# A four-part reordering in a one-core transformer kernel: keys before the first queries, other room for the last probabilities, operand steps queued with the splits, a deferred factor

## The chip, the cores and the metric

The kernel runs on one core of a Trainium2 chip. The metric is the device time of one execution in microseconds (us). TensorE is called PE, VectorE DVE, ScalarE ACT, GpSimd POOL and SyncE SP, as in the profile.

## The reference

x has 2 sequences of 1024 tokens of width 512. Four blocks follow one another, each with a layer norm ahead of it and a residual around it: a chunked linear attention with decay, a feed-forward block with 8-bit codes as weights, a softmax attention, and the same feed-forward block again.

```
x = x + attn_a(_layernorm(x))
x = x + ffn(_layernorm(x))
x = x + attn_b(_layernorm(x))
x = x + ffn(_layernorm(x))
# attn_a, per chunk of 128 tokens and head of 128:
k = k / max(norm(k), 1e-12)
attn = (q k^T) * beta * decay                 # causal
y = attn v + (q state) * chunk_decay
state = state * total_decay + v^T (k * beta * decay_to_end)
# attn_b: softmax((Q K^T) / sqrt(512)) V, then W_o
# ffn:    W_down (silu(W_gate x) * (W_up x)), W = (codes - 128) * scale
```

## The kernel before, in words

**Products.** A float32 product is made as three products of a rounded type: each operand is split into a high and a low part. `split` (L83 to L86) casts the high part on ACT (L85) and subtracts it from the source on DVE, or on POOL where it is told so, for the low part (L86). `mm3` (L97 to L100) issues high by high (L98), high by low (L99) and low by high (L100). `load_split` (L88) loads a 128x512 block of a weight into a stage tile and splits it. `product_operands` and `weight_product` make two products of weights: M from WqT and WkT at the very start, and V from WvT and Wo at the end of the first attention. `spill` (L181) takes such a product from PSUM: for each of its four blocks it makes two tiles, splits into them and writes both to DRAM; for M the two tiles of each block have the tag sWk, which has two buffers and which the keys of the first attention use too.

**First attention.** 16 tiles of 128 tokens, in four stages of four. At the start, while M is made, tiles 0 to 3 are normalised and turned on PE (`ln_tile`, pxT_a at L133). Then come load_wab (L367, the gates' weights), the constants, Wq from a staged tile (the room y of the pool for turned x), M's spill, the four heads of queries of stage 0 (`q_head`, pq) with tiles 4 to 7 normalised between them, Wk and Wv, and `kv_tile(0)` (L536): the keys and values of a tile, pWk and pWv, biased into sWk and sWv on DVE (L547). For each tile, `k_norm` (L551) squares the keys on ACT (sq, L558), sums them (ss, L560) and bounds the sum (L561) on DVE, takes a power on POOL (s, L563), multiplies it by two factors on DVE (L564, L569) and by the keys on POOL (kw, L571). `scores` (L576) turns the keys on PE (pkT, L581, copied to kT on ACT, L583), makes the state's increment (pd, L594, from sWv and kw), the scores (pS, L609), and weighs them by the factor s and the decay into at (L613). `chunk_out` (L619) makes the output: pl (L628) from sWv and at, pg (L633) from the state. The decay's rows reach all partitions by loads of row (L531), and dec is their exponential (L523).

**What runs beside it.** `fill` puts into each tile's step the normalisation of later stages, the down weights of the feed-forward block, the loads of V's operands, and steps of `combine` (L244), which makes sums and differences of blocks of x (B and T, split by L86 and differenced at L259) for the products of the feed-forward block. V's product is made in the last two tiles' steps (pV, L98 to L100).

**Second attention, its end.** `probs_T` (L997) turns a tile of probabilities: tile 14 on PE (split at once), the others on DVE (py), which then write it to DRAM and read it back in four transfers into the low tile ptl, to be split in place by `probs_split` (L1031). pth is the high part. ptl and pth have two buffers, and so has pe, the tile of probabilities before it is turned. `out_b` (L1038) makes the output pob from these and the values. After the last tile's turned probabilities come six steps of combine("g", 0), then out_b of tiles 13 and 14, the loads of the next block's weights wcg (`stationary`), and out_b of 15.

**What sets the order.** The program is written as one thread; a scheduler with a timeline of its own puts each engine's instructions into one fixed order, by what is free in its timeline and by the program's order. `behind` (L76) says that instructions stand after given others in that order. Each engine then runs its list in order and waits at the head of it. A tile that takes a buffer waits until all readers of the buffer's earlier tile are done, a transfer out included.

Of the kernel before, what the change touches and what calls it, by code (L numbers as in the profile page):

```python
# [16 lines left out]
P = 128  # L17
D = 512
KD = D // P
T = 1024  # L20
# [14 lines left out]
def hybrid_block_kernel(ctx: ExitStack, tc: tile.TileContext, a, out):  # L35
# [313 lines left out]
    with ExitStack() as actx:  # L349
# [2 lines left out]
        a3 = actx.enter_context(tc.tile_pool(name="attn_a3", bufs=3))  # L352
        sp = actx.enter_context(tc.tile_pool(name="stage", bufs=4))

        normed, key_copy = {}, []
        xTa, aba, gta, sca, qTa, kva, ata, deca, sta, rowa, facta = ({} for _ in range(11))
        wqkv = {}
        wab = a1.tile([P, KD, 48], F32R, name="wab")
# [6 lines left out]
                nc.sync.dma_start(out=dst, in_=a["rows"][n:m].partition_broadcast(P))  # L365

        def load_wab():  # L367
            stg = sp.tile([P, 512], F32, tag="stg", name="stg_ab")
            ab = stg[:, 0 : KD * 8].rearrange("p (k c) -> p k c", k=KD)
            nc.sync.dma_start(out=ab, in_=a["Wab"].rearrange("(k p) c -> p k c", p=P))  # L370
            for c in (0, 32):
                split(wab[:, :, c : c + 8], wab[:, :, c + 8 : c + 16], ab)
            nc.vector.tensor_scalar(
                wab[:, :, 16:32], ident[:, 0 : KD * 16].rearrange("p (k c) -> p k c", k=KD), 0.0, None, ALU.mult
            )

        def load_wqkv(nm, staged=None):
            two = [slot(f"{nm}{n}") for n in range(2)]
            wqkv[nm] = [two[k // 2][:, k % 2 * 1024 : (k % 2 + 1) * 1024] for k in range(KD)]
            for k in range(KD):  # L380
                w, eng = wqkv[nm][k], nc.gpsimd if k % 2 else None
                if staged is None:
                    load_split(w, sp, a[nm][k * P : (k + 1) * P, :], f"{nm}{k}", eng)
                else:
                    split(w[:, 0:512], w[:, 512:1024], staged[:, k], eng)

        xa = [x_in[t * P : (t + 1) * P, :] for t in range(NT)]

# [144 lines left out]
                in_=cl_d[st][i * H : (i + 1) * H, :].rearrange("h c -> (h c)").partition_broadcast(P),  # L533
            )

        def kv_tile(t):  # L536
            st, i = divmod(t, ST)
            xh, xl = xTa[st]
            cs = bass.ts(i, P)
            kv = []  # L540
            for nm, b in (("Wk", bk_b), ("Wv", bv_b)):
                ps = psum(f"p{nm}{t}")
                for k in range(KD):
                    w = wqkv[nm][k]
                    mm3(ps, xh[:, k, cs], xl[:, k, cs], w[:, 0:512], w[:, 512:1024], k == 0, k == KD - 1)
                o = tl(f"s{nm}", t, pool=a3 if nm == "Wv" else ap)
                nc.vector.tensor_tensor(o.rearrange("p h d -> p (h d)"), ps, b, ALU.add)  # L547
                kv.append(o)
            kva[t] = kv

        def k_norm(t, after=None):  # L551

            st, i = divmod(t, ST)
            beta, ec, _ = sca[st]
            kf, v = kva[t]
            sq = tl("sq", t)
            with tc.issue_after(after) if after is not None else nullcontext():
                squared = nc.scalar.activation(sq, kf, AF.Square).ins  # L558
            ss = mp.tile([P, H], F32, tag="ss", name=f"ss{t}")
            nc.vector.tensor_reduce(ss, sq, AX.X, ALU.add)  # L560
            nc.vector.tensor_scalar(ss, ss, 1e-24, None, ALU.max)  # L561
            s1 = mp.tile([P, H], F32, tag="s1", name=f"s1{t}")
            nc.gpsimd.tensor_tensor(s1, ss, mhalf.to_broadcast([P, H]), ALU.pow)  # L563
            scaled = nc.vector.tensor_tensor(s1, s1, beta[:, i, :], ALU.mult).ins  # L564
            normed[t] = squared, scaled
            kw = None
            if t % NC < NC - 1:
                s2 = mp.tile([P, H], F32, tag="s2", name=f"s2{t}")
                scaled = nc.vector.tensor_tensor(s2, s1, ec[:, 1, i, :], ALU.mult).ins  # L569
                kw = tl("kw", t)  # L570
                weighted = nc.gpsimd.tensor_tensor(kw, kf, s2.unsqueeze(2).to_broadcast([P, H, P]), ALU.mult)  # L571
                normed[t] = squared, scaled, weighted.ins
            kva[t] = kf, kw, v
            facta[t] = s1
# [74 lines left out]
        for k in range(KD):  # L649
            if k + 1 < KD:  # L650
                loads.append(product_operands(sp, a["WqT"], a["WkT"], "M", k + 1))
            if k < 2:
                xs += [load_x(xa[t], f"a{t}", "xres" if t > 1 else "xin") for t in (2 * k, 2 * k + 1)]
            if k == 2:

                staged = yp.tile([P, 4, KD, ST, 32], F32, tag="y", name="y_Wq")
                staged = staged.rearrange("p k a b c -> p k (a b c)")
                for m in range(KD):
                    wq_loaded = nc.sync.dma_start(out=staged[:, m], in_=a["Wq"][m * P : (m + 1) * P, :]).ins
            pm, end = next(prep)  # L660
            with behind((end, loads[-1][2])):
                for t in ((), (0, 1), (2, 3), ())[k]:
                    ln_tile(t)
        load_wab()
        load_consts()
        with behind((*normed_x, *parts[-2:])):
            load_wqkv("Wq", staged)
        spill(ap, ("sWk",), pm, m_d, "M")
        for i in range(4):
            q_head(0, i)  # L670
            with behind((wq_loaded,)):
                ln_tile(4 + i)
        load_wqkv("Wk")
        load_wqkv("Wv")
        kv_tile(0)
        decays(0)
        k_norm(0)

# [19 lines left out]
        for t in range(NT):  # L698
            if t + 4 < NT:
                q_head(*divmod(t + 4, ST))  # L700
            if t == 0:
                decay_rows(0)
                load_row(0)
                load_row(1)
            load_row(t + 1)
            if (t + 2) % ST:
                load_row(t + 2)
            if t + 1 < NT:
                kv_tile(t + 1)
            weighed = scores(t)  # L710
            if t + 1 < NT:
                with behind((*normed[t + 1][2:], *key_copy)):
                    decay(t + 1)
            with behind(normed.get(t + 1, (weighed,))):
                for step in fill[t]:
                    step()
                if 1 <= t <= KH:
                    down_weights(sp, t - 1)
                for n in {NT - 3: (0,), NT - 2: (1, 2), NT - 1: (3,)}.get(t, ()):
                    loads.append(product_operands(sp, a["WvT"], a["Wo"], "V", n))  # L720
                if t == NT - 3:
                    first_codes = [
                        load_codes(xp, "xn", a["wgu"][0][:, n * 512 : (n + 1) * 512], f"cf0_{n}") for n in range(2)
                    ]
                if t == NT - 2:
                    wcs.append(stationary(0, "f0", loaded=first_codes))
                for n in range(3 if NT - 4 <= t < NT - 1 else 0):
                    moving.pop(0)()
                if t == NT - 1:
                    wcs.append(stationary(1, "f0", (sp, "stg")))  # L730
            if t == NT - 2:
                prep = weight_product(loads, "V")
            if t >= NT - 2:
                next(prep)
# [145 lines left out]
    with ExitStack() as bctx:  # L880
# [116 lines left out]
        def probs_T(b, i):  # L997
# [4 lines left out]
            if t == NT - 2:  # L1002
# [3 lines left out]
                for s in range(2):  # L1006
                    ps = psum(f"ppt{t}_{s}").rearrange("p (k c) -> p k c", k=4)
                    ks = slice(s * 4, s * 4 + 4)
                    for k in range(4):
                        n = (s * 4 + k) * P  # L1010
                        ends[s] = nc.tensor.transpose(ps[:, k, :], pe[:, n : n + P], ident).ins
                    split(hi[:, ks], lo[:, ks], ps)
                ptT[t] = hi, lo, ri
                return
            y = b1.tile([P, T], F32, tag="py", name=f"py{t}")
            nc.vector.transpose(y, pe)

            nc.sync.dma_start(
                out=p_d[i].rearrange("k p f -> p k f"), in_=y.rearrange("p (k f) -> p k f", k=NK)
# [1 line left out]
            lo = bp.tile([P, NK, P], F32R, tag="ptl", name=f"ptl{t}")  # L1021
            hi = bp.tile([P, NK, P], F32R, tag="pth", name=f"pth{t}")
            raw = lo.bitcast(F32)
            placed = p_d[i].rearrange("k (c j) (r q) -> r j (k c) q", c=4, r=4)
            for r in range(4):
                nc.sync.dma_start(
                    out=raw[32 * r : 32 * (r + 1)].rearrange("p k (c q) -> p (k c) q", c=4), in_=placed[r]
                )
            ptT[t] = hi, lo, ri

        def probs_split(b, i, after):  # L1031
            hi, lo, _ = ptT[b * NK + i]
            with behind(after):
                for s in range(2):
                    ks = slice(s * 4, s * 4 + 4)
                    split(hi[:, ks], lo[:, ks], lo[:, ks].bitcast(F32))

        def out_b(b, i):  # L1038
            t = b * NK + i
            hi, lo, ri = ptT[t]  # L1040
            xr = xp.tile([P, D], F32, tag="xres", name=f"xrb{t}")
            nc.sync.dma_start(out=xr, in_=x2[t])
            po = psum(f"pob{t}")
# [6 lines left out]
        def v_tile(b, kt):  # L1050
# [8 lines left out]
            split(h_, l_, ps)  # L1059
            vs[b, kt] = h_, l_  # L1060

        qs, QA, heads, pes, ptT, vs, last, summed = {}, {}, {}, {}, {}, {}, [], []

        def do(steps, n):
# [92 lines left out]
        array(probs_T, 1, 6)  # L1157
        probs_T(1, 7)
        probs_split(1, 7, last)
        do(moving, 6)  # L1160
        array(out_b, 1, 5)
        array(out_b, 1, 6)
        wcs = [stationary(n, "g0") for n in range(2)]
# [66 lines left out]
```

## Time and profile before

| | |
|---|---|
| median of 3 runs | 955.0 us (953.75 to 956.41) |
| the profiled execution's own time | 955.52 us |
| its span, first to last instruction | 953.8 us |
| mean granted clock of TensorE | 0.996 |
| PE busy | 935.7 us, 98% of the span |
| DVE, ACT, POOL busy | 724.0, 409.8, 223.0 us |
| bytes moved | 162.18 MB, mean 170 GB/s |

The span is cut into busy and idle time for each engine; what an engine waited for at the end of an idle stretch is named as its releaser. The time outside the span, 1.7 us in this execution, is the start and end of the program. A stage is read from its own stretch of the trace, not from the shares of the whole span.

### The profile page before, as it was taken

The page shows a single profiled execution, that of the slowest core. Times are in us where ns is not written, and L with a number is a line of the kernel's source. Part 1 is how long each engine was busy: PE and PEld are TensorE (multiplying, and loading weights), DVE is VectorE, ACT ScalarE, POOL GpSimd, SP SyncE. Part 2 cuts the span into 40 slices and gives each one's busy share as a digit, 9 for nine tenths or more (in the row PEclk, how much of TensorE's full clock was granted, in tenths as well). Part 3 has the DMA queues.
Part 4 walks back from the last instruction along what each step waited for, and adds up shares of the span by engine and source line. Part 5 has one row for each costly group of instructions (what it writes and reads, how often), then busy time and mean ns, then how long its engine had stood idle before and what let it go on. Part 6 is the DMA issues. An engine that isn't in the chain of part 4 may idle for free.

```text
span 953.8 us, 13227 instructions
## 1 busy us (share of the span) xinstructions
PE 935.7 (98%) x4402; PEld 775.3 (81%) x4402; DVE 724.0 (76%) x1457; ACT 409.8 (43%) x795; POOL 223.0 (23%) x318
## 2 busy tenths in 40 slices
PE   8999999998999999999999999999988999999998
PEld 6788888897888878888888888888867788888887
DVE  7657767778999699788947879469873967976655
ACT  4654343344665344454324444145341543534421
POOL 5433323443364011120120402040400261001100
PEclk9999999999999999999999999999999999999999
DMA  9526356665898358632842778226884762573112
GB/s 319 168 95 181 133 140 156 190 187 157 293 370 293 90 188 279 182 83 85 288 113 56 182 172 241 79 45 150 208 236 142 288 192 48 185 263 125 40 61 95
DMA packets 215861, 162.18 MB, mean 170 GB/s; under 512 B 150960, under 2 KB 166640, under 8 KB 215792
## 3 DMA queue, kind: packets, MB, share of 16 engines
q1 hardware_dynamic: 213488, 156.61, 54.0%
q0 software_dynamic: 2304, 4.72, 2.3%
q8 instruction: 35, 0.57, 0.2%
q14 instruction: 34, 0.28, 0.1%
HBM read 104.76 MB, written 41.84 MB: 154 GB/s over the span
## 4 chain that ended last, share of the span: by engine, by line
PE 89%; DVE 3%; DMA 2%; SPq 2%; ACT 1%; issue 1%; POOL 0%; DVEq 0%; ACTq 0%; POOLq 0%
PE pog L852 4%; PE pog L851 4%; PE pof L852 4%; PE pof L851 4%; PE pVg L339 4%; PE pZg L339 4%; PE pXg L339 4%; PE pXf L339 4%; PE pVf L339 4%; PE pZf L339 4%; PE pob L100 3%; PE pob L98 3%; PE pob L99 3%; PE psV L949 2%; PE psZ L949 2%; PE psX L949 2%
## 5 line engine op out<-in xcount | busy, mean ns | idle before, releaser
L851 PE MATMUL pog<-wdg,hsg 128*128 128x512 f32 (+1 forms) x165 | 60.3, 375 | 0.0
L852 PE MATMUL pog<-wdg,hsg 128*128 128x512 f32 (+1 forms) x165 | 60.2, 375 | 0.0
L851 PE MATMUL pof<-wdf,hsf 128*128 128x512 f32 x154 | 59.1, 390 | 0.7 <-ACT hsf L85 0.7
L852 PE MATMUL pof<-wdf,hsf 128*128 128x512 f32 x154 | 58.9, 390 | 0.0
L98 PE MATMUL pob<-vh,pth 128*128 128x512 f32 x128 | 50.8, 397 | 4.3 <-ACT pth L85 4.3
L100 PE MATMUL pob<-vh,ptl 128*128 128x512 f32 x128 | 50.6, 395 | 2.1 <-DVE ptl L86 2.1
L99 PE MATMUL pob<-vl,pth 128*128 128x512 f32 x128 | 50.4, 394 | 0.0
L86 POOL TENSOR_TENSOR hsg<-sgg,hsg 128x128 fp32r<-128x128 f32 x40 | 19.1, 498 | 125.7 <-ACT hsg L85 125.6
L123 POOL TENSOR_TENSOR rs_g<-ve_g,mhalf 128x1 f32<-128x1 f32 x16 | 13.0, 816 | 144.5 <-DVE ve_g L121 144.5
L339 PE MATMUL pXg<-B_g,wcg 128*128 128x512 f32 x176 | 46.6, 389 | 0.0
L339 PE MATMUL pVg<-T_g,wcg 128*128 128x512 f32 x176 | 46.4, 389 | 0.0
L339 PE MATMUL pVf<-T_f,wcf 128*128 128x512 f32 x176 | 46.3, 389 | 0.0
L339 PE MATMUL pXf<-B_f,wcf 128*128 128x512 f32 x176 | 45.4, 390 | 0.0
L123 POOL TENSOR_TENSOR rs_b<-ve_b,mhalf 128x1 f32<-128x1 f32 x16 | 12.7, 802 | 136.8 <-DVE ve_b L121 132.6
L211 POOL DMA_DIRECT2D xT_g<-y_g x48 | 30.9, 652 | 39.7 <-DVE T_b L86 28.5
L339 PEld LDWEIGHTS pVg<-T_g,wcg 128*128 128x128 f32 x176 | 33.0, 188 | 6.9
L339 PEld LDWEIGHTS pXg<-B_g,wcg 128*128 128x128 f32 x176 | 33.0, 188 | 6.9
L339 PEld LDWEIGHTS pVf<-T_f,wcf 128*128 128x128 f32 x176 | 33.1, 188 | 6.9
L339 PEld LDWEIGHTS pXf<-B_f,wcf 128*128 128x128 f32 x176 | 32.9, 188 | 7.0 <-issue 0.3
L851 PEld LDWEIGHTS pog<-wdg,hsg 128*128 128x128 f32 x165 | 31.1, 188 | 5.7
L852 PEld LDWEIGHTS pog<-wdg,hsg 128*128 128x128 f32 x165 | 31.0, 188 | 5.6
L851 PEld LDWEIGHTS pof<-wdf,hsf 128*128 128x128 f32 x154 | 28.9, 188 | 7.1 <-ACT hsf L85 1.1
(333 smaller groups left out, 2738.1 us busy)
## 6 DMA issues: line engine op xcount, KB each, us to landing
wcg<-wc SPq DMA_DIRECT2D x22, 896.0 KB, 6.0
wc<-wcf SPq DMA_DIRECT2D x11, 896.0 KB, 5.9
wcf<-wc SPq DMA_DIRECT2D x11, 896.0 KB, 6.4
p<-py SPq DMA_DIRECT2D x15, 512.0 KB, 3.6
ptl<-p SPq DMA_DIRECT2D x60, 128.0 KB, 3.0
xin_a<-in_x SPq DMA_DIRECT2D x16, 256.0 KB, 4.4
xra<-in_x SPq DMA_DIRECT2D x16, 256.0 KB, 2.8
row<-cl SPq DMA_DIRECT2D x16, 256.0 KB, 3.7
```

The costliest lines, as they stand in the source:

```text
L86: return c.ins, (eng or nc.vector).tensor_tensor(lo, src, hi.bitcast(F32), ALU.subtract).ins
L98: nc.tensor.matmul(ps, lhs_hi, rhs_hi, start=first, stop=False)
L99: nc.tensor.matmul(ps, lhs_hi, rhs_lo, start=False, stop=False)
L100: end = nc.tensor.matmul(ps, lhs_lo, rhs_hi, start=False, stop=last).ins
L123: nc.gpsimd.tensor_tensor(rs, ve, mhalf, ALU.pow)
L211: (nc.sync if sync else nc.gpsimd).dma_start(out=xf[32 * b : 32 * (b + 1), :, c, :], in_=y[32 * c : 32 * (c + 1), b].rearrange("p k i q -> ...
L339: nc.tensor.matmul(ps, w[:, m, k * P : (k + 1) * P], o[:, s, k, :], start=first and k == 0 and s == 0, stop=k == 1 and s == 1, skip_group_ ...
L851: nc.tensor.matmul(ps, hs[i][0][:, j], wd[j][:, ds], start=j == 0, stop=False)
L852: nc.tensor.matmul(ps, hs[i][1][:, j], wd[j][:, ds], start=False, stop=j == KH - 1)
L949: ends[nm] = nc.tensor.matmul(ps, o[:, i, k], w[:, j, k], start=first and k == 0 and i + j == 0, stop=k == 1 and i == 1, skip_group_check= ...
```

## The change

It has four parts. At the start, the staged room holds Wk and not Wq; load_wab has a tile of its own and is called when the third block of M is made; the keys of tile 0 (`kv_part(0, "Wk")`) stand behind the last product of M (`end`), ahead of the first queries; Wq is loaded through the stage tiles. `kv_tile` becomes two calls of `kv_part`. M's spill comes after the keys of tile 0. `k_norm` is cut in two, and of the last tile the second half (`k_factor`) is called in the step of tile 14, behind the last four splits of V's operands. The last tile's probabilities return from DRAM into a tile raw in the room of pe, not into ptl. The six steps of combine("g", 0) stand behind `splits`, the splits of tiles 13 and 14 and the turning of tile 15.

```
@@ -352,7 +352,7 @@
         a3 = actx.enter_context(tc.tile_pool(name="attn_a3", bufs=3))
         sp = actx.enter_context(tc.tile_pool(name="stage", bufs=4))
 
-        normed, key_copy = {}, []
+        normed, key_copy, late_norm = {}, [], []
         xTa, aba, gta, sca, qTa, kva, ata, deca, sta, rowa, facta = ({} for _ in range(11))
         wqkv = {}
         wab = a1.tile([P, KD, 48], F32R, name="wab")
@@ -365,8 +365,7 @@
                 nc.sync.dma_start(out=dst, in_=a["rows"][n:m].partition_broadcast(P))
 
         def load_wab():
-            stg = sp.tile([P, 512], F32, tag="stg", name="stg_ab")
-            ab = stg[:, 0 : KD * 8].rearrange("p (k c) -> p k c", k=KD)
+            ab = a1.tile([P, KD, 8], F32, name="stg_ab")
             nc.sync.dma_start(out=ab, in_=a["Wab"].rearrange("(k p) c -> p k c", p=P))
             for c in (0, 32):
                 split(wab[:, :, c : c + 8], wab[:, :, c + 8 : c + 16], ab)
@@ -380,9 +379,10 @@
             for k in range(KD):
                 w, eng = wqkv[nm][k], nc.gpsimd if k % 2 else None
                 if staged is None:
-                    load_split(w, sp, a[nm][k * P : (k + 1) * P, :], f"{nm}{k}", eng)
+                    _, load = load_split(w, sp, a[nm][k * P : (k + 1) * P, :], f"{nm}{k}", eng)
                 else:
                     split(w[:, 0:512], w[:, 512:1024], staged[:, k], eng)
+            return load if staged is None else None
 
         xa = [x_in[t * P : (t + 1) * P, :] for t in range(NT)]
 
@@ -533,29 +533,40 @@
                 in_=cl_d[st][i * H : (i + 1) * H, :].rearrange("h c -> (h c)").partition_broadcast(P),
             )
 
-        def kv_tile(t):
+        def kv_part(t, nm):
             st, i = divmod(t, ST)
             xh, xl = xTa[st]
             cs = bass.ts(i, P)
-            kv = []
-            for nm, b in (("Wk", bk_b), ("Wv", bv_b)):
-                ps = psum(f"p{nm}{t}")
-                for k in range(KD):
-                    w = wqkv[nm][k]
-                    mm3(ps, xh[:, k, cs], xl[:, k, cs], w[:, 0:512], w[:, 512:1024], k == 0, k == KD - 1)
-                o = tl(f"s{nm}", t, pool=a3 if nm == "Wv" else ap)
-                nc.vector.tensor_tensor(o.rearrange("p h d -> p (h d)"), ps, b, ALU.add)
-                kv.append(o)
-            kva[t] = kv
+            ps = psum(f"p{nm}{t}")
+            for k in range(KD):
+                w = wqkv[nm][k]
+                mm3(ps, xh[:, k, cs], xl[:, k, cs], w[:, 0:512], w[:, 512:1024], k == 0, k == KD - 1)
+            o = tl(f"s{nm}", t, pool=a3 if nm == "Wv" else ap)
+            b = bv_b if nm == "Wv" else bk_b
+            nc.vector.tensor_tensor(o.rearrange("p h d -> p (h d)"), ps, b, ALU.add)
+            kva[t] = (*kva.get(t, ()), o)
+
+        def kv_tile(t):
+            kv_part(t, "Wk")
+            kv_part(t, "Wv")
 
         def k_norm(t, after=None):
 
-            st, i = divmod(t, ST)
-            beta, ec, _ = sca[st]
             kf, v = kva[t]
             sq = tl("sq", t)
             with tc.issue_after(after) if after is not None else nullcontext():
                 squared = nc.scalar.activation(sq, kf, AF.Square).ins
+            normed[t] = (squared,)
+            if t == NT - 1:
+                late_norm.append(lambda: k_factor(t, sq))
+            else:
+                k_factor(t, sq)
+
+        def k_factor(t, sq):
+            st, i = divmod(t, ST)
+            beta, ec, _ = sca[st]
+            kf, v = kva[t]
+            squared = normed[t][0]
             ss = mp.tile([P, H], F32, tag="ss", name=f"ss{t}")
             nc.vector.tensor_reduce(ss, sq, AX.X, ALU.add)
             nc.vector.tensor_scalar(ss, ss, 1e-24, None, ALU.max)
@@ -653,26 +664,28 @@
                 xs += [load_x(xa[t], f"a{t}", "xres" if t > 1 else "xin") for t in (2 * k, 2 * k + 1)]
             if k == 2:
 
-                staged = yp.tile([P, 4, KD, ST, 32], F32, tag="y", name="y_Wq")
+                staged = yp.tile([P, 4, KD, ST, 32], F32, tag="y", name="y_Wk")
                 staged = staged.rearrange("p k a b c -> p k (a b c)")
                 for m in range(KD):
-                    wq_loaded = nc.sync.dma_start(out=staged[:, m], in_=a["Wq"][m * P : (m + 1) * P, :]).ins
+                    nc.sync.dma_start(out=staged[:, m], in_=a["Wk"][m * P : (m + 1) * P, :])
+                load_wab()
             pm, end = next(prep)
             with behind((end, loads[-1][2])):
                 for t in ((), (0, 1), (2, 3), ())[k]:
                     ln_tile(t)
-        load_wab()
         load_consts()
         with behind((*normed_x, *parts[-2:])):
-            load_wqkv("Wq", staged)
+            load_wqkv("Wk", staged)
+        with behind((end,)):
+            kv_part(0, "Wk")
+        wq_loaded = load_wqkv("Wq")
         spill(ap, ("sWk",), pm, m_d, "M")
         for i in range(4):
             q_head(0, i)
             with behind((wq_loaded,)):
                 ln_tile(4 + i)
-        load_wqkv("Wk")
         load_wqkv("Wv")
-        kv_tile(0)
+        kv_part(0, "Wv")
         decays(0)
         k_norm(0)
 
@@ -718,6 +731,9 @@
                     down_weights(sp, t - 1)
                 for n in {NT - 3: (0,), NT - 2: (1, 2), NT - 1: (3,)}.get(t, ()):
                     loads.append(product_operands(sp, a["WvT"], a["Wo"], "V", n))
+                if t == NT - 2:
+                    with behind(parts[-4:]):
+                        late_norm.pop()()
                 if t == NT - 3:
                     first_codes = [
                         load_codes(xp, "xn", a["wgu"][0][:, n * 512 : (n + 1) * 512], f"cf0_{n}") for n in range(2)
@@ -1009,11 +1025,13 @@
                     for k in range(4):
                         n = (s * 4 + k) * P
                         ends[s] = nc.tensor.transpose(ps[:, k, :], pe[:, n : n + P], ident).ins
-                    split(hi[:, ks], lo[:, ks], ps)
-                ptT[t] = hi, lo, ri
+                    splits.extend(split(hi[:, ks], lo[:, ks], ps))
+                ptT[t] = hi, lo, lo.bitcast(F32), ri
                 return
             y = b1.tile([P, T], F32, tag="py", name=f"py{t}")
-            nc.vector.transpose(y, pe)
+            turned = nc.vector.transpose(y, pe).ins
+            if t == NT - 1:
+                splits.append(turned)
 
             nc.sync.dma_start(
                 out=p_d[i].rearrange("k p f -> p k f"), in_=y.rearrange("p (k f) -> p k f", k=NK)
@@ -1021,23 +1039,28 @@
             lo = bp.tile([P, NK, P], F32R, tag="ptl", name=f"ptl{t}")
             hi = bp.tile([P, NK, P], F32R, tag="pth", name=f"pth{t}")
             raw = lo.bitcast(F32)
+            if t == NT - 1:
+
+                raw = bp.tile([P, T], F32, tag="pe", name=f"raw{t}").rearrange("p (k c) -> p k c", k=NK)
             placed = p_d[i].rearrange("k (c j) (r q) -> r j (k c) q", c=4, r=4)
             for r in range(4):
                 nc.sync.dma_start(
                     out=raw[32 * r : 32 * (r + 1)].rearrange("p k (c q) -> p (k c) q", c=4), in_=placed[r]
                 )
-            ptT[t] = hi, lo, ri
+            ptT[t] = hi, lo, raw, ri
 
         def probs_split(b, i, after):
-            hi, lo, _ = ptT[b * NK + i]
+            hi, lo, raw, _ = ptT[b * NK + i]
             with behind(after):
                 for s in range(2):
                     ks = slice(s * 4, s * 4 + 4)
-                    split(hi[:, ks], lo[:, ks], lo[:, ks].bitcast(F32))
+                    done = split(hi[:, ks], lo[:, ks], raw[:, ks])
+                    if b * NK + i == NT - 3:
+                        splits.extend(done)
 
         def out_b(b, i):
             t = b * NK + i
-            hi, lo, ri = ptT[t]
+            hi, lo, _, ri = ptT[t]
             xr = xp.tile([P, D], F32, tag="xres", name=f"xrb{t}")
             nc.sync.dma_start(out=xr, in_=x2[t])
             po = psum(f"pob{t}")
@@ -1059,6 +1082,7 @@
             split(h_, l_, ps)
             vs[b, kt] = h_, l_
 
+        splits = []
         qs, QA, heads, pes, ptT, vs, last, summed = {}, {}, {}, {}, {}, {}, [], []
 
         def do(steps, n):
@@ -1157,7 +1181,8 @@
         array(probs_T, 1, 6)
         probs_T(1, 7)
         probs_split(1, 7, last)
-        do(moving, 6)
+        with behind(splits):
+            do(moving, 6)
         array(out_b, 1, 5)
         array(out_b, 1, 6)
         wcs = [stationary(n, "g0") for n in range(2)]

```

## The prediction, made before the run

> **What bounds the kernel now.** First the page's busy shares and its chain that ended last.
>
> ```profile
> PE 935.7 (98%) x4402; PEld 775.3 (81%) x4402; DVE 724.0 (76%) x1457; ACT 409.8 (43%) x795; POOL 223.0 (23%) x318
> ...
> PE 89%; DVE 3%; DMA 2%; SPq 2%; ACT 1%; issue 1%; POOL 0%; DVEq 0%; ACTq 0%; POOLq 0%
> ```
>
> TensorE (PE) works 98% of the span. So only two things count: what PE waits for, and at what clock it runs. The view of PE's waits comes next (engine, line, whom it waited for: us, times, longest).
>
> ```profile
> PE pob L98 <- ACT pth L85: 4.3, 2, 2.5
> PE pV L99 <- DVE V L86: 2.3, 1, 2.3
> PE pob L100 <- DVE ptl L86: 2.1, 1, 2.1
> PE pab L401 <- DVE wab L86: 1.5, 1, 1.5
> ...
> PE pl L628 <- DVE at L613: 0.5, 1, 0.5
> ```
>
> They sit, by the instruction starts, at 19.5 us (pab, 1.46), 228.4 (pl, 0.54), 231.8 (pV, 2.26), 703.7 (pob, 1.75), 706.1 (pob, 2.07) and 720.5 (pob, 2.52): 10.6 us, and the change aims at each. Then the table of stretches (us, PE busy ... PEclk, DMA share, GB/s):
>
> ```profile
> 231.80:233.94 2.14, 0.03 (x1) 0.00 (x0) 2.14 (x3) 0.00 (x0) 1.61 (x2) 1.00 0.57 166
> 233.94:237.36 3.42, 3.27 (x8) 2.59 (x9) 3.42 (x7) 0.95 (x1) 0.00 (x0) 0.50 0.82 258
> ...
> 708.40:711.81 3.41, 3.41 (x9) 2.64 (x9) 2.68 (x4) 0.69 (x1) 0.00 (x0) 0.50 1.01 334
> ```
>
> After two of the stops the granted clock is 0.50 for 3.41 us; some eight 128x512 products go at 0.427 us apart instead of 0.2275, so each costs 8 x 0.20 = 1.6 us more. All that the change can win is 10.6 + 3.2 = 13.8 us.
>
> Last, the path of tile 1 through the first attention, which the change touches without naming it: the chain, and the timeline of GpSimd (POOL).
>
> ```profile
> 52.50 0.44 PE pkT L581 x4
> ...
> 63.72 0.44 PE pkT L581 x4
> 64.16 0.89 PE pd L594 x8
> ```
>
> ```profile
> 56.89 1.01 POOL L563 TENSOR_TENSOR s<-ss,mhalf 128x4 f32<-128x4 f32 x1 [1.14 <-DVE ss L561]
> ...
> 58.72 1.04 POOL L571 TENSOR_TENSOR kw<-sWk,s 128x512 f32<-128x512 f32 x1 [0.82 <-DVE s L569]
> ```
>
> kw1 is ready at 59.8, and PE wants it (pd1) at 64.0: 4.2 us of slack.
>
> **What the Trainium skill says.** "TensorE: Matmul & The Clock Gate", What's actually happening: the clock is halved after an idle window of 3413 ns, and the windows run free of the kernel. The trace agrees: both drops last 3.413 us and lie 139 windows apart; the windows before them were about 62% and 70% idle; one 46% idle had no drop. [...] the last two writes of M landed 1.98 and 1.97 us after issue. "SBUF — State Buffer", SBUF: two separate sides: a DVE operation with two SBUF inputs and a GpSimd operation lock each other out. The trace agrees: a Wq split took 1.76 us on DVE beside GpSimd's, against 0.69 alone.
>
> **The change, part by part.**
>
> Start. pWk0 (12 products, 2.73 us) can begin when pM ends, 19.36, because Wk is now the staged weight. pab follows at 21.64 with its operands ready (wab 19.6). That fills the 1.46. But Wq, now loaded late, lands at 18.5 to 20.5, and its DVE splits meet GpSimd's: 21.7 and 23.45. Behind them on DVE stand three bn_stats, sWk0, ab0, another bn_stats (0.6 to 0.69 each) and xn_a4, done at 28.0; PE wants it at 26.64. A wait of 1.4 replaces the 1.46. **Gain 0.7**: between 0.2 and, without the lock, 1.6.
>
> Spill of M. M0..M3 (two tiles each, written to DRAM) share two buffers, A and B, with sWk. Before, they stood ahead of sWk0, and all left by 41.2. Now sWk0 takes A first. The order of instructions gives M0_0 B, M0_1 A (after pkT0 has read sWk0), M1 B and A, M2, M3, and only then sWk1 and sWk2. Each reuse waits for a write to land. With 0.68 for a split and 2.0 for a write: pkT0 ends near 52.5; M0_1 to 53.7, landed 55.7; M1_1, behind four at0 on DVE, to 56.6, landed 58.7; M2_0 (behind qT1_1 on ACT) and M2_1 to 59.8, landed 61.9; M3_0 on ACT to 61.7, behind a table load of 1.28 and two logarithms that stand behind M2_1, landed 63.7; M3_1 to 63.0, landed 64.9. sWk1 63.9 to 64.5, so pkT1 is 1.2 late. Then sWv2, sWk2 (65.7), ss1 (66.5), the power 1.01 (67.6), and on GpSimd the power of tile 2 ahead of kw1 (68.6), kw1 1.04: 69.7. pd1 starts at 69.7, not 64.0: **loss 5.7**. With immediate ACT turns it is 69.4, so 5.4; with a longer landing 6.5. Queued behind on DVE are ss, at1 and tile 8's normalisation; on SP, whose writes wait for M0_1 to M3_1, are row2, cd1, row3, and the next x tiles. The turned x of stage 2 (16 transfers that end at 88.5, used at 92.3) moves by about the same 5 to 6.5 us, so I add nothing. PE stands 5.9 of 6.3 us: a window is idle and the clock halves. Averaged over where the window falls, 2.45 to 4.2 us of half speed remain: **loss 1.6** (1.2 to 2.1).
>
> Factor of tile 15 deferred. V1 and V2 splits move ahead of ss15, T2 and T3; the ACT casts T2, T3 move ahead of kT15. V1's low halves end 229.3; PE arrives at 228.1: 1.1 idle. The power for s115 now stands on GpSimd behind wcf0_2's two (whose codes come by DMA): pow to about 238.3, at15 1.13 for four, PE there at 237.5: 1.0 to 1.85 idle. The old 0.54 + 2.26 + 1.6 = 4.4 become 2.5: **gain 2.2** (1.8 to 2.6; none, if the codes come 2 us later).
>
> Steps queued with the splits. pth13 goes ahead of B22's cast (1.05) on ACT, ending a microsecond earlier: the 1.75 becomes 0.7. ptl13 goes ahead of L259 and B22 on DVE: 2.07 becomes 1.0. 1.7 idle over 2.45 us seldom fills half a window: the half clock goes (5 in 6). 1.05 + 1.07 + 1.4: **gain 3.5** (2.1 to 3.7).
>
> Other room for tile 15's probabilities. Their four reads no longer wait for pob13 to free ptl. They are issued near 709 to 711.5, once the write (3.5 to 4.2) has landed, land near 714.5, and pth15 is done by 716.5: the 2.52 goes. But on SP they stand ahead of wcg0_0, issued at 711.5, not 706.4; at 6.0 median it lands at 717.5, wanted at 716.9: 0 to 1.1. **Gain 2.0** (1.5 to 2.5). Wab's own tile: nothing, its 16 KB load is in the same queue; were it late by 1 us, pab would show that.
>
> Sum: -0.7 + 5.7 + 1.6 - 2.2 - 3.5 - 2.0 = **-1.1 us**. The profiled run took 955.5 (span 953.8 and 1.7 around it), the median 955.0: 954.4 and 953.9. I say 954.
>
> **Rivals.**
>
> A, likeliest (0.62): as summed, the tail's gains eaten by the spill. Own range, from the ends above (start 0.2 to 1.6, spill 5.4 to 6.5 with clock 1.2 to 2.1, the others 5.4 to 8.8): 951 to 958.
>
> B (0.22): the spill's chain costs PE nothing, as if it were off the path. For: 4.2 us of slack, and the queue of transfers is empty from 52.6 to 55 and 58 to 63. Against: three landings of 2.0 alone use 6. Then 953.9 - 7.3 = 946.6.
>
> C (0.16), the other side: a write of M takes as long as those did beside loads, 3.7 in the median, not 2.0:
>
> ```profile
> L186 SPq DMA_DIRECT2D m<-M x4: 327/355/438, 21.5 to 39.3; - x4
> ...
> DMA to landing us min/median/max: 2.0/3.7/4.8
> ```
>
> Row2's load is issued just ahead of M1_0's write. Three hops x 1.7 = 5.1 more: 959. It is slower by over 0.3% (2.9 us) from 3.3 us a landing, 3 x 1.3 = 3.9 more. Against: only row2 shares the queue, and those writes had eight loads beside them.
>
> **Numbers.** 0.3% is 2.9 us, about what a measurement of this kernel can tell from no change. B is faster; of A, 0.11 lies under 952.1, 0.50 within, 0.01 above; C is slower. Faster 0.33, same 0.50, slower 0.17. The range: 946.5 (B's value) to 958 (A's upper end, C left out).
>
> **What would show it.** PE's waits: pd <- GpSimd kw of 4 to 5 us near 65 to 70, pkT <- DVE sWk about 1.2, and a clock of 0.5 near 70; M's writes between 54 and 65. No pab wait, but pxT_a <- xn_a of 0 to 1.4 near 27. At 228 to 240 two waits of about 1 to 1.9 and a full clock; at 703 to 706 waits of 0.7 and 1.0; at 720 none for pth, perhaps one for wcg. If pd1 starts before 66, the spill step is wrong and B stands; if the waits at 703 keep their size, the steps didn't move.

## The result, and the profile after

| | before | after |
|---|---|---|
| median | 955.85 us (8 runs, 953.75 to 957.78) | 959.35 us (8 runs, 958.02 to 961.6) |
| ratio | | 1.0038, 95% interval 1.0024 to 1.0053 |
| profiled execution, span | 953.8 us | 958.8 us |

The change made the kernel 3.5 us slower by the medians, 5.0 us by the profiled executions. The prediction was 954.0, with a range of 946.5 to 958. (L numbers are each kernel's own: the pd of L594 before is L605 after.)

First the page's busy shares and the chain that ended last, of the kernel after.

```profile
PE 936.6 (98%) x4402; PEld 776.3 (81%) x4402; DVE 728.9 (76%) x1457; ACT 408.6 (43%) x793; POOL 222.1 (23%) x318
...
PE 81%; DVE 7%; DMA 6%; ACT 2%; issue 1%; POOL 1%; SPq 1%; ACTq 0%; DVEq 0%; POOLq 0%
```

PE does the same work. But the chain leaves it for DVE and DMA: 7 and 6%, where it was 3 and 2. The view of PE's waits says where.

```profile
PE pd L605 <- POOL kw L582: 6.3, 2, 4.4
PE pl L639 <- DVE at L624: 2.5, 1, 2.5
PE pkT L592 <- DVE sWk L546: 1.3, 1, 1.3
PE pob L98 <- ACT pth L85: 1.2, 1, 1.2
...
PE pxT_a L133 <- DVE ve_a L121: 1.0, 1, 1.0
PE pV L99 <- DVE V L86: 1.0, 1, 1.0
...
PE pob L100 <- DVE ptl L86: 0.7, 1, 0.7
```

pab's 1.5 has gone, the 2.5 before the last pob has gone, and the two waits at the end of the second attention are 1.2 and 0.7, not 1.8 and 2.1. In their place stand pkT and pd at 64 to 71 us (1.3 and 4.4), another pd at 229 (1.9), and pl at 248 (2.5). The stretches (us, PE busy ... PEclk, DMA share, GB/s) show the price of the two at 64 to 71:

```profile
66.30:70.73 4.43, 0.01 (x2) 0.00 (x1) 3.99 (x12) 3.01 (x4) 3.06 (x4) 0.84 0.18 69
69.27:76.10 6.83, 5.37 (x25) 5.37 (x26) 5.19 (x14) 2.66 (x9) 5.95 (x8) 0.50 0.34 94
```

PE stands for 4.43 us, and from 69.27 the clock is 0.50 for 6.83 us, two windows and not one.

The starts of the same products in both traces split the 5.0 us. Each line says how many us longer a stretch is after than before, beside the term of the prediction. The number behind a product is its tile; pof and pog are the down products of the first and the second feed-forward block:

| stretch | predicted | profiled |
|---|---|---|
| start to pkT0 | -0.7 | +0.61 |
| pkT0 to pd1 (spill) | +5.7 | +6.12 |
| pd1 to pkT2 (clock) | +1.6 | +2.62 |
| pkT2 to pkT14 | 0 | -0.37 |
| pkT14 to the first pof (deferral) | -2.2 | +1.34 |
| first pof to first pog (splits, own room) | -5.5 | -5.30 |
| the rest | 0 | -0.04 |
| sum | -1.1 | +5.0 |

### The profile page after: what moved, and what is told of

The parts are those of the page before. It is cut to its first block, busy times and chain, and to the rows that moved or that the text cites. A ratio compares the mean times of both kernels' runs of the same rounds, so it can differ in the third digit from the quotient of the medians.

```text
span 958.8 us, 13209 instructions
## 1 busy us (share of the span) xinstructions
PE 936.6 (98%) x4402; PEld 776.3 (81%) x4402; DVE 728.9 (76%) x1457; ACT 408.6 (43%) x793; POOL 222.1 (23%) x318
## 4 chain that ended last, share of the span: by engine, by line
PE 81%; DVE 7%; DMA 6%; ACT 2%; issue 1%; POOL 1%; SPq 1%; ACTq 0%; DVEq 0%; POOLq 0%
PE pog L868 4%; PE pog L867 4%; PE pZg L339 4%; PE pVg L339 4%; PE pXg L339 4%; PE pVf L339 4%; PE pZf L339 3%; PE pXf L339 3%; PE pob L100 3%; PE pof L867 3%; PE pob L98 3%; PE pob L99 3%; PE pof L868 3%; PE pYg L339 2%; PE psV L965 2%; PE psZ L965 2%
```

## The experiments

The theory after the result: M's eight tiles go one after another through two buffers, each waiting for the landing of a write, and sWk1 stands at the end of that row; the tail gains what was forecast; the deferral gains nothing, since the power on POOL stands behind codes. The rival: the loss comes from the keys moved ahead or from the lateness of everything behind them, and the deferral itself works.

Each experiment was timed beside the kernel before on the same chip. The median of before was 954.3 to 955.8 us there, so the ratio to it counts (with its 95% interval), and a gain or loss in us is worked out from the ratio; it can differ by about a microsecond from that of the medians.

**1. M's spill in other rooms.** All parts of the change, with

```
-        spill(ap, ("sWk",), pm, m_d, "M")
+        spill(ap, ("sq", "kT", "kw", "sdec"), pm, m_d, "M")
```

> The changed kernel, with M's spill in the rooms of sq, kT, kw and sdec (two buffers each, one room per block) and not in the room of sWk. Theory (the two shared buffers make M's eight tiles, and then sWk1, wait for one another's writes): no wait of pkT or pd near 65 to 75 us, no halved clock there, M written before 45 us; 8.7 us less than the changed kernel (6.1 of waits and 2.6 of clock), less up to 2.4 given back where M's four low parts now stand ahead of tile 4's normalisation: 950.5 to 953. Rival (the wait comes from the keys moved ahead or from the two powers on GpSimd ahead of kw, not from the buffers): within 2 us of the changed kernel's 959.4.

Measured: 955.02 us (14 runs), ratio to before 0.9994, 0.9982 to 1.0005. PE's waits in this kernel:

```profile
PE pxT_a L133 <- DVE ve_a L121: 4.1, 1, 4.1
PE pl L639 <- DVE at L624: 2.3, 1, 2.3
PE pd L605 <- POOL kw L582: 1.4, 1, 1.4
```

The waits of pkT and pd at 64 to 71 and the halved clock there are gone (pd's 1.4 is tile 14's, at 225). The keys still stand ahead of the queries here, so the two buffers were the cause. But only 4.3 of 8.7 us came back, and the expectation was missed by 2: a wait of 4.1 stands at 26.9, with a halved window after it, and another halved window follows the wait of pl. DVE's timeline shows why (start, us):

```profile
20.92 1.27 DVE L86 TENSOR_TENSOR M<-pM,M 128x512 fp32r<-128x512 f32 x2
22.11 1.72 DVE L86 TENSOR_TENSOR Wq<-stg_Wq,Wq 128x512 fp32r<-128x512 f32 x1
23.76 1.27 DVE L86 TENSOR_TENSOR M<-pM,M 128x512 fp32r<-128x512 f32 x2
...
25.56 1.27 DVE L117 BATCH_NORM_STATS2 bn_a<-xin_a 128x6 f32<-128x512 f32 x2
```

Freed of their wait, M's four low parts (2 x 1.27) run ahead of tile 4's normalisation, and PE waits for that.

**2. The tail alone.** The kernel before, with the edits of probs_T, probs_split and `with behind(splits)` only.

> The kernel before with two parts only: the last probabilities' own room, and the operand steps behind the splits. Theory: all of the gain seen at the end of the changed kernel is theirs: 5.3 us faster than before, 950.5. Rival (that gain depends on the 10 us by which everything before it was late): half or less, 953 or more.

Measured: 948.97 us (6 runs), 0.9933, 0.9915 to 0.9951: 6.4 us faster. The theory holds; the gain doesn't need the lateness.

**3. The deferral alone.** The kernel before, with k_factor and late_norm only.

> The kernel before with the deferred factor of tile 15 only. Theory (the power on GpSimd stands behind codes whose transfer is issued late): the wait of the last pl on at is 2 to 2.5 us, the wait of V and the halved clock go, the sum is within 1 us of before: 955 to 957. Rival (the loss seen there in the changed kernel came from the stage being 9 us late against its transfers, so the deferral itself does what was forecast): 2.2 us faster, 953.6.

Measured: 955.0 us (22 runs), 0.9995, 0.9985 to 1.0005: nothing. The last pl waits 2.24 us. The rival falls: without any lateness of the stage the deferral gains nothing either.

**4. The start alone.** The kernel before, with the staged Wk, load_wab's own tile, kv_part, the late Wq and the spill behind it.

> The kernel before with the start only (keys ahead of queries, Wq through the stage tiles, M's spill after the keys in sWk's room). Theory: the waits of pkT and pd with the halved clock are all here: 8 to 9.5 us slower than before, 964 to 965. Rival (part of that loss came from the other parts): under 6 us.

Measured: 961.37 us (6 runs), 1.0063, 1.0044 to 1.0082: 6.0 us slower, less than the theory has and at the edge of the rival. The waits are there (pkT 1.31, pd 4.62, half clock 6.83 us), and at pkT2 the trace is 9.5 us behind that of before. 2 of those are regained where the last pob waits 0.53 and not 2.52, and 1.6 where the clock isn't halved after V's wait.

**5. Tail and a repaired start.** No deferral. Of the start:

```
-        spill(ap, ("sWk",), pm, m_d, "M")
...
         load_wqkv("Wv")
+        with behind(normed_x[-1:]):
+            spill(ap, ("sq", "kT", "kw", "sdec"), pm, m_d, "M")
         kv_part(0, "Wv")
```

> The start and the tail of the change, with two edits of the start: M's spill has the rooms of sq, kT, kw and sdec, and its low parts stand behind tile 7's normalisation; no deferral. Theory: neither the wait of pkT and pd near 65 to 75 nor the 4.1 us wait of pxT_a that the first repair showed; the start is worth 0 to 1 us, the tail 6.3: 948 to 949 where before is 955.3. Rival (the start costs for another reason, the late Wq): 951 or more, with a wait of 2 us or more before 30 us.

Measured: 949.81 us (8 runs), 0.9952, 0.9930 to 0.9973. pxT_a waits 1.13 at 27.6; pkT and pd don't wait near 65 to 75, so the rival's wait isn't there. But on a before of 955.3 this ratio is 950.7, which lies between the two expectations: 1.8 us behind the tail alone by the ratios, within their intervals. Whether the repaired start costs or brings something is not settled here.

**6. The deferral with the power early.** As 3, with

```
-                    with behind(parts[-4:]):
+                    with behind(parts[-4:-2]):
```

> The deferral alone as in the third experiment, but behind V's block 1 only: the sum ss of tile 15 stands between V1 and at14, and its power on GpSimd ahead of wcf0_2. Theory (the power behind the codes made the last pl wait 2.24 us): that wait falls below 0.7, and the kernel is 1.5 us or more faster than with the deferral as it was, 953.5. Rival (at15 is late for another reason, DVE's queue of V2, T2 and T3): the wait stays above 1.5 us and the time at 955.

Measured: 955.55 us (22 runs), 1.0008, 0.9998 to 1.0018. pl still waits 2.39, and the clock halves behind it. My theory of this wait, that the codes alone make it, fell: the power now stands ahead of them and ends 0.9 us earlier in its stage than in run 3 (19.2 and 20.1 us after pkT14), but at15 starts 0.7 later (21.7 and 21.0). The timelines of POOL and DVE in this kernel:

```profile
236.37 3.06 POOL L575 TENSOR_TENSOR s<-ss,mhalf 128x4 f32<-128x4 f32 x1 [1.74 <-DVE ss L573]
```

```profile
236.13 0.15 DVE L573 TENSOR_SCALAR ss<-ss 128x4 f32<-128x4 f32 x1
236.20 2.35 DVE L86 TENSOR_TENSOR T_f<-xT_f,T_f 128x1024 fp32r<-128x1024 f32 x2
239.46 0.69 DVE L576 TENSOR_TENSOR s<-s,beta 128x4 f32<-128x4 f32 x1 [0.91 <-POOL s L575]
...
240.86 1.13 DVE L649 SCALAR_TENSOR_TENSOR xra<-pg,ec,xra 128x128 f32<-128x128 f32 x4
241.90 1.12 DVE L625 SCALAR_TENSOR_TENSOR at<-pS,s,dec 128x128 f32<-128x128 f32 x4
```

The power, 1.02 us elsewhere, takes 3.06: it starts while DVE is in two splits of 128x1024 with both inputs in SBUF (2.35 us), and ends 0.88 after them, while DVE stands idle for it. It is the lock that the prediction had named for Wq, and had not looked for here. And between s and at15 DVE adds to xra twice (L641, L649; 1.8 us), which in run 3 it did ahead of s: the rival has a share in this wait too, with other operations than it named.

**7. The operand steps behind the splits, alone.** The kernel before, with the `splits` edits only.

> The kernel before with the operand steps behind the splits only. Theory: the waits of pob at 704 and 706 become 1.2 and 0.7 and the halved clock goes, 2.0 and up to 1.6 us: 952 to 953.3. The 2.5 us wait of the last pob stays. Rival (the six steps, queued later, make the next block's first products wait as long): 955.

Measured: 950.15 us (7 runs), 0.9945, 0.9925 to 0.9965: 5.2 us, more than expected. The waits are 1.22 and 0.74, the clock stays full there, and the last pob doesn't wait, though its room is as before: in this kernel its four reads are issued from 712.92, ahead of the loads of wcg, and not from 715.09 behind them. So the edit moved more than the two waits that it was made for.

**8. The last probabilities' own room, alone.** The kernel before, with `raw` in the room of pe only.

> The kernel before with the last probabilities' own room only. Theory: the 2.5 us wait of the last pob goes, and the first weights of the next block, whose transfer now stands behind the four reads, are waited for by at most 1.1 us: 952.8 to 954. Rival (that transfer takes the whole of it back): 955 or more.

Measured: 953.59 us (22 runs), 0.9987, 0.9977 to 0.9997: 1.2 us. The wait of the last pob is gone, and wcg is not waited for. That wait is 2.52 us in the trace of before, 1.02 in run 6, 0.53 in run 4 and 0.19 in run 3: the trace of before had a large one.

**9. The changed kernel without the deferral.**

> The changed kernel without the deferred factor: start, own room and splits as changed. Theory: the parts add up, the start costs 6 to 8.5 us, the tail gains 6.3, and the deferral is worth 0 to 1 either way: 955 to 957, so that the changed kernel's 959.4 holds 2 to 4 us of the deferral in that company. Rival (the deferral costs nothing there, and the gain of the tail is smaller beside the changed start): 959 or more.

Measured: 957.19 us (15 runs), 1.0033, 1.0022 to 1.0044. The median lies between the two expectations, but the changed kernel's 959.35 was timed beside a before of 955.85, and on that this ratio gives 959.0: the rival's number. The ratios leave the deferral 0.05% here, within the intervals, and not 2 to 4 us. Beside the tail (0.9933) the start costs 1.0033 - 0.9933, 1.0% or 9.6 us; alone it cost 6.0. End of interval against end of interval these are 6.8 to 12.3 and 4.2 to 7.8 us, which overlap.

**10. Tail and deferral.** The changed kernel without its start.

> The kernel before with own room, splits and deferral, without the start. Theory: the deferral adds about 1 us of waiting before the last pl and saves 1.6 where the clock would have halved after V's wait: within 1.5 us of the tail alone, 948 to 950.5. Rival (the deferral is worth its forecast 2.2): 946.8.

Measured: 950.55 us (13 runs), 0.9961, 0.9950 to 0.9971, just above the theory's range; the tail alone had 0.9933. End of interval set against end of interval, the deferral costs between nothing and 5 us; the 2.2 gained is excluded.

**11. Tail and deferral, with the power free.** As 10, with

```
-                    with behind(parts[-4:]):
+                    with behind(parts[-4:-2]):
...
-                    moving.pop(0)()
+                    with behind(normed[NT - 1][1:2] if t == NT - 2 else ()):
+                        moving.pop(0)()
```

> As the run with tail and deferral, with two edits: the factor stands behind V's block 1 only, and the last three operand steps before it (L259, T2, T3) stand behind its product. Theory (the power was held for 3.06 us by the two 128x1024 splits of T2 and T3 on VectorE, against 1.02 alone): the power takes 1.0 us, the last pl waits under 1 us, and the sum is 1 to 2 us less than with tail and deferral as it was: 947. Rival (T2 and T3, now late, are waited for by the next products): the wait moves to pYf or pZf and the time stays at 949.

Measured: 947.86 us (5 runs), 0.9935, 0.9923 to 0.9948. The power on POOL, and PE's wait for at:

```profile
234.39 1.01 POOL L575 TENSOR_TENSOR s<-ss,mhalf 128x4 f32<-128x4 f32 x1
```

```profile
PE pl L640 <- DVE at L625: 1.4, 2, 0.8
```

The power takes 1.01, V isn't waited for at all, pl waits 0.55 for at14, as before, and 0.81 for at15 (they were 0.98 for V and 2.53 for at15 in the changed kernel). The length of the power is what the theory of the lock says, and the wait doesn't move on to pYf or pZf, products of the feed-forward block. But the edit also takes the 2.35 us of T2 and T3 out of DVE's list ahead of at15. How much of the wait was the lock and how much DVE's list, no run separates.

**12. All four parts, repaired.** The start of 5, the deferral of 11, the tail.

> All four parts of the change, each with its repair: M's spill in the rooms of sq, kT, kw and sdec with its low parts behind tile 7's normalisation; the factor of tile 15 behind V's block 1 and the last three operand steps behind its product. Theory: no wait over 1.3 us except at the very start, no halved clock at 69 or 234, the time that of the last run or up to 1 us less, since the repaired start fills pab's 1.46 with 1.1 of its own: 947 to 948 where before is 955. Rival (the parts disturb one another, as the deferral did in the changed kernel): 950 or more.

Measured: 947.65 us (5 runs), 0.9924, 0.9910 to 0.9937: 7.3 us faster than before and some 11 faster than the change as it was. PE's longest waits:

```profile
PE pl L639 <- DVE at L624: 1.4, 2, 0.8
PE pob L98 <- ACT pth L85: 1.2, 1, 1.2
...
PE pxT_a L133 <- DVE ve_a L121: 1.1, 1, 1.1
```

No window has the halved clock from 6.6 us until the program's last microsecond. The interval overlaps that of the tail alone (0.9915 to 0.9951): what the repaired start and deferral add is not settled by the times. No single wait after the program's start is longer than 1.22 us.

## Why the prediction was wrong, step by step

**Spill of M: right in mechanism and size.** It said that pkT1 would be 1.2 late and pd1 would start at 69.7, 5.7 later. Measured 1.30, and 70.73; without the 0.6 by which the start was late, 6.1 later. The lines of M in the kernel after (duration in ns; first and last start):

```profile
L86 DVE TENSOR_TENSOR M<-pM,M x4: 680/691/691, 53.8 to 63.0; 128x512 fp32r<-128x512 f32 x4
L186 SPq DMA_DIRECT2D m<-M x4: 319/320/323, 54.5 to 63.8; - x4
...
  DMA m<-M: 1.9, 3
```

The four low parts are spread over 53.8 to 63.7, and the row waits three times for a landing. The end of the chain (start, us, what):

```profile
62.85 1.97 DMA m<-M
...
64.91 0.69 DVE sWk L546
...
66.80 0.61 DVE ss L571
...
67.67 1.48 POOL s L574 x2
69.16 0.48 issue
69.64 1.05 POOL kw L582
```

This is the row that the prediction had written down, with M3_0's landing at 64.8 and not 63.7: the load of row2, issued 0.43 earlier, stood ahead of M1_0's write (3.49 us to land, not 2.0). Rival B, in which the chain costs nothing, is out by run 1, where other rooms remove both waits. Rival C, a landing of 3.7 for every write, isn't what happened: the others of this row took 2.0 to 2.8. That the total came out at C's 959 is luck.

**Clock after the stop: the mechanism right, the size off.** "Loss 1.6 (1.2 to 2.1)" was 2.62. The stops cover 87% of the window from 65.86 and 43% of the next one, which was itself at half speed, and the window after that was at half speed too: 6.83 us, where the prediction, averaging over where the window falls, had 2.45 to 4.2. Runs 4 and 9 have the same two windows behind these stops.

**Factor of tile 15: the step that failed.** It said "gain 2.2 (1.8 to 2.6; none, if the codes come 2 us later)". Its own numbers give less: 4.4 less 2.5 is 1.9. V's idle was right, 0.98 for 1.1. The wait of pl on at15 was not: "1.0 to 1.85" was 2.53. The power was to be done at "about 238.3", which is 247.3 with the 9.0 us by which the stage was late. DVE and POOL in the kernel after:

```profile
243.79 0.67 DVE L571 TENSOR_REDUCE ss<-sq 128x4 f32<-128x512 f32 x1
244.38 2.35 DVE L86 TENSOR_TENSOR T_f<-xT_f,T_f 128x1024 fp32r<-128x1024 f32 x2
246.65 0.16 DVE L572 TENSOR_SCALAR ss<-ss 128x4 f32<-128x4 f32 x1
```

```profile
247.16 0.74 POOL L322 TENSOR_TENSOR wcf<-wcf 128x256 fp32r<-128x256 f32 x1 [3.73 <-ACT wcf L305]
247.85 0.74 POOL L324 TENSOR_TENSOR wcf<-wcf 128x256 fp32r<-128x256 f32 x1
248.54 1.02 POOL L574 TENSOR_TENSOR s<-ss,mhalf 128x4 f32<-128x4 f32 x1
```

It was done at 249.56, 2.3 later. Two things hold it: on DVE the splits of T2 and T3 stand between the sum ss and its bound, so that ss is ready at 246.8 only, and on POOL the power then stands for 1.7 us behind codes that landed at 245.04. Run 6 takes the codes out of its way, but there the power meets T2 and T3 on DVE and at15 stands behind the two additions to xra; the wait is as long. Run 11 takes T2 and T3 away as well, and the wait falls to 0.81. No run moves T2 and T3 alone.

So V and at15 were waited for 3.51 us in sum, where 2.5 was forecast and the old order had 2.80 (0.54 and 2.26): the deferral could save nothing but the half clock behind V's wait. Of the 3.5 us between forecast and trace in this stretch, 1.0 is this wait, 0.3 the slip in the sum, 0.3 a new wait of pYf for POOL, and 0.4 is not traced. The other 1.5 is pd of tile 14 (1.86 for 0.36), which the prediction left out: in the trace its power stands on POOL behind row's select, which waited for a transfer that landed at 226.99, 1.25 before pkT14, where before it was 2.75 ahead. That wait is 0.36 to 1.29 us in the seven profiles without the deferral, 0.95 to 1.86 in the five in which the power is not free, and under 0.2 and 0.67 in runs 11 and 12; what sets it was not tried.

How little the deferral gives shows best in the time from pkT14 to the first pof: 93.4 us in the mean of the seven profiles without it (92.4 to 94.6), 94.6 in the four with it as it was, 90.6 in the two with the free power.

**Half clock saved: counted as certain, but it hangs on where the windows fall.** V's wait of 2.26 is in seven profiles; in four of them the clock halves after it, in three (runs 2, 4, 9) not. The 1.6 that the deferral was to save was in the trace of before, but in four of seven only, and the new wait of pl brought a half clock of its own in two of five (runs 1 and 6). And the prediction gave the half clock at the end 5 chances in 6 to go with waits of 0.7 and 1.0. In nine profiles with 1.2 and 0.7 it goes in four; in the kernel after it stayed. With the old 1.8 to 2.2 and 2.1 it came in five of five.

The windows can be laid from each trace's own half-speed stretches, 3.413 us apart, and PE's idle share in each be counted. At full clock, between 7 us and the last 20 us of the 14 profiles, no window idle for 46% or less was followed by half speed, all sixteen idle for 57.4% or more were, and of the ten between 49 and 57% four were (49% in run 10, 53 in the kernel after, 55 in run 9, 56 in run 5) and six were not (49 in run 10, 52 in runs 4 and 8, 54 in run 9, 56 in the kernel after, 57 in run 2). A few products can be missing from a trace, so these shares are not exact. The 1.2 and 0.7 fill 49 to 57% of one window in the five profiles where the clock halves, and at most 30 to 46% in the four where it doesn't.

**Start: -0.7 became +0.6.** Of that, 0.87 is there at the first turning on PE, before the change touches anything on that path: the third block for M landed at 9.91, not 9.04, at the same issue. The twelve experiments have that turning at 11.07 to 11.73, the trace of before at 10.92 and that of after at 11.79: the one was early, the other late. From there to pkT0 the change gains 0.26: pab's 1.46 is filled, and pxT_a waits 1.02 for the 1.4 forecast.

**Tail: right as a sum, partly by luck.** 3.5 and 2.0 were forecast, 5.3 appeared, and alone the parts gave 5.2 and 1.2. The 1.4 for the half clock did not come in this trace; the waits give 4.4 (1.86 and 2.52), and the other 0.9 lies behind the first product of the next block, where nothing was forecast. The 2.52 of the last pob was taken from a trace in which it is at its largest.

So the three wrong terms (start 1.3, clock 1.0, deferral 3.5) are 5.8 of the 6.1 us between forecast and profile; the spill's excess of 0.4 and the 0.4 regained behind it cancel. What stays open is whether the start truly costs more beside the tail (9.6 us by the ratios, 7.9 by the spans of the profiles of runs 9 and 2) than alone (6.0). In the trace of run 4 a part of its loss is given back where the last pob waits less, and beside the tail that wait isn't there to be shortened; that this is the reason is not shown.

## What to carry to other kernels

When an allocation is moved past another in the same room, write out who gets which buffer next, down to the next user that has nothing to do with the change: here the keys of tile 1 paid for a spill of weights. A term that a single trace shows (a halved window, one wait before the last tile) is a draw; ask what would have to move a little for it not to be there, for the clock where its windows would begin, and put it into the sum by that chance. And when a short operation on GpSimd becomes the last thing that is waited for, look at both its queue and at what VectorE does in the same microseconds.

## What the runs showed of the hardware that was not expected

A power of 128x4 on GpSimd took 3.06 us instead of 1.02 beside two VectorE splits of 128x1024 that ran one right after the other (2.35 us together), and ended 0.88 us after the second: in this one case it did not come in between the two. A write of 256 KB from SBUF to DRAM landed 1.97 us after its issue where no other transfer was issued just ahead of it, and 3.49 to 3.99 us where a load of the same size was (the kernel after, runs 4 and 9). The clock was halved after windows of 3.413 us in which PE had stood for about half the time (49% in run 10, 53% in the kernel after); between 49 and 57% it went either way, and at full clock it was never halved after 46% or less.
